# Taking the 32 largest scores from maxima of four instead of maxima of two

## The chip, the cores and the metric

The kernel runs on one core of a Trainium2 chip. The metric is device time in microseconds of one execution; lower is better. A core has five engines with queues of their own: TensorE (PE, matrix products), VectorE (DVE), ScalarE (ACT), GpSimd (POOL) and SyncE (SP, which issues most transfers). [...]

## The reference, cut to what matters

A gated cross-attention block over 8 batches of 512 text rows, with 1024 context rows per batch, four heads of width 32, is followed by a state-space mixing, a feed-forward layer and a routed layer of eight experts. The change touches only how attention picks its scores:

```
scores = einsum("bthd,bghd->bhtg", Q, K) / sqrt(32)      # 8 x 4 x 512 rows of 1024
topv, topi = top_k(scores, 32)
probs = softmax(topv)
attn = zeros_like(scores).at[..., topi].set(probs)
attn_mean = attn.mean(over heads)
```

Per row of 1024 scores one needs the 32nd largest value (the threshold), the largest one (for the exponent), and the sum of the exponentials of those at or above the threshold.

## The kernel before, in words

The rows of a batch are four tiles of 128 rows (t), one row per partition. A step of attention treats one tile and two heads, i = 0 and 1: 8 batches x 4 tiles x 2 pairs of heads are 64 steps, or 128 heads of one tile. In a step ScalarE copies the scores of the two heads from PSUM into tiles sc[0] and sc[1] of 128 x 1024 float32. Then the selection follows:

- VectorE takes the maximum of the left and the right half of a score row (line 943), 512 pair maxima, into the first half of a tile mn.
- GpSimd finds the smaller one of each pair: it adds the two halves as 32-bit whole numbers (line 945) and subtracts the maximum (line 946). The result is the bit pattern of the minimum, in the second half of mn.
- VectorE draws the 32 largest pair maxima in four rounds of MAX8 (the eight largest of a row), with MATCH_REPLACE8 between them (those eight replaced by a very low number, line 956, in a tile left).
- One MAX8 over the 512 pair minima (line 965) takes their eight largest. The eighth largest of these eight and of the last eight of the first 32 is the threshold th. It is the right one as long as no more than eight of a row's 32 are pair minima.

Afterwards ScalarE has made the exponentials e of all scores; VectorE multiplies them with (score >= threshold) and sums them (line 977, an operation with two SBUF tiles as inputs); ScalarE counts the chosen ones through a sum of signs, scales by the reciprocal of the sum, and GpSimd adds the heads up in acc (line 984). At the end of the program the counts are looked at: if a row has not exactly 32, a general version of the whole computation runs behind.

Buffers set part of the order: two tiles mn, two left and two e for all steps, so that a step's mn becomes free with the MAX8 over its second half, and four score tiles.

Beside the attention of batch b, the mixing, feed-forward and routed work of batch b - 1 runs on the same engines. The kernel does not write its instructions out in the order of the program: it notes them all with an estimated cost (function `time`, line 137) and their dependencies and buffers, and a list planner (function `order`, line 220) puts them into each engine's queue by estimated start and then by place in the program, shifted for attention and scores by the constants of line 337. So each engine's order is fixed before the kernel runs and follows estimates, not the chip. In TensorE's planned gaps the kernel puts filler matmuls (idle). Every planned instruction is recorded under line 326 in the profile; the tiles' names tell them apart: mn, left, top (the maxima drawn), t (the last MAX8 of 16), e, acc, sc.

Of the kernel before, what the change touches and what calls it, by code (L numbers as in the profile page):

```python
# [12 lines left out]
F32 = mybir.dt.float32  # L13
# [3 lines left out]
I32 = mybir.dt.int32  # L17
AF = mybir.ActivationFunctionType
ALU = mybir.AluOpType
# [3 lines left out]
P = 128  # L23
# [326 lines left out]
def tile_kernel(ctx: ExitStack, tc: tile.TileContext, a: dict, out: bass.AP):  # L350
# [3 lines left out]
    G, DV = cx.shape[1:]  # L354
    H, DH = 4, 32
    KTOP = 32
    HID = a["L0_xattn_W1"].shape[1]
    NST = a["L0_xattn_A_re"].shape[1]
    NE, _, NI = a["L0_ffn_rt_gate"].shape
# [4 lines left out]

    L = T // 2
    NL, NFFT = L // P, 2 * L
    SCALE = 1.0 / float(np.sqrt(np.float32(DH)))


# [15 lines left out]
    pk = ctx.enter_context(tc.tile_pool(name="pk", bufs=2))  # L385
# [10 lines left out]
    V, S, GP, TE, SY = (plan.engine(n, e) for n, e in (  # L396
        ("DVE", nc.vector), ("ACT", nc.scalar), ("POOL", nc.gpsimd), ("PE", nc.tensor), ("SP", nc.sync)))
# [495 lines left out]
    def scores(b, s, t, h0):  # L893

        plan.lead += LEAD_S
        n = f"{b}_{t}_{h0}"
        sc = [pq.tile([P, G], F32, tag="s", name=f"sc{n}_{i}") for i in range(2)]
        for q in range(G // 512):
            qs = slice(q * 512, (q + 1) * 512)
            pS = []  # L900
            for i in range(2):
                hp = slice((h0 + i) * DH, (h0 + i + 1) * DH)
                pS.append(ps_sc.tile([P, 512], F32, tag="sc", name=f"pS{n}_{i}_{q}", bufs=2))
                TE.matmul(pS[i], s.qT[hp, t * P : (t + 1) * P], s.kT[hp, qs], start=True, stop=True)
            for i in range(2):
                S.copy(sc[i][:, qs], pS[i])
        plan.lead -= LEAD_S
        return sc

    def attention(states):  # L910


        steps = [(b, t, h0) for b in range(B) for t in range(NT) for h0 in range(0, H, 2)]
        ahead = scores(0, states[0], 0, 0)
        behind = None
        for k, (b, t, h0) in enumerate(steps):
            s, sc = states[b], ahead
            if k + 1 < len(steps):
                b_, t_, h_ = steps[k + 1]
                for _ in states[b_].prep:  # L920
                    pass
                ahead = scores(b_, states[b_], t_, h_)
            if (t, h0) == (0, 0):


                s.uT = pk.tile([DK + 1, 2, T], F32, tag="uT", name=f"uT{b}")
                GP.memset(s.uT[DK : DK + 1, 0, :], 1.0)
            if h0 == 0:
                acc = pk.tile([P, G], F32, tag="acc", name=f"acc{b}_{t}")
            n = f"{b}_{t}_{h0}"  # L930

            top = pk.tile([P, 2, KTOP + 8], F32, tag="top", name="top" + n)
            sm = pk.tile([P, 5, 2], F32, tag="sm", name="sm" + n)
            nm, nb, na, su, ri = (sm[:, k_, :] for k_ in range(5))
            e_, mn = [], []
            for i in range(2):
                m_ = pk.tile([P, 2, G // 2], F32, tag="mn", name=f"mn{n}_{i}")  # L940
                mn.append(m_)
                lo, hi = sc[i][:, : G // 2], sc[i][:, G // 2 :]
                V.tensor_tensor(m_[:, 0], lo, hi, ALU.max)
                mi = m_.bitcast(I32)
                GP.tensor_tensor(mi[:, 1], lo.bitcast(I32), hi.bitcast(I32), ALU.add)
                GP.tensor_tensor(mi[:, 1], mi[:, 1], mi[:, 0], ALU.subtract)
            for i in range(2):
                for r in range(KTOP // 8):
                    t8 = top[:, i, r * 8 : r * 8 + 8]
                    src = mn[i][:, 0] if r == 0 else left  # L950
                    V.max(t8, src)
                    if r == 0:
                        S.activation(nm[:, i : i + 1], t8[:, 0:1], AF.Copy, scale=-SCALE)
                        left = pk.tile([P, G // 2], F32, tag="left", name=f"left{n}_{i}")
                    if r < KTOP // 8 - 1:
                        V.match_replace(left, t8, src, TAKEN)
                e_.append(pk.tile([P, G], F32, tag="e", name=f"e{n}_{i}"))
                S.activation(e_[i], sc[i], AF.Exp, bias=nm[:, i : i + 1], scale=SCALE)
                if i == 0:
                    yield  # L960
                    if behind is not None:
                        behind()
                        behind = None
            for i in range(2):
                V.max(top[:, i, KTOP:], mn[i][:, 1])
            t8 = pk.tile([P, 2, 8], F32, tag="t8", name="t8" + n)
            for i in range(2):
                V.max(t8[:, i, :], top[:, i, KTOP - 8 :])
            th = t8[:, :, 7]

            S.activation(na, th, AF.Abs, scale=EPS32)
            for i in range(2):
                S.activation(nb[:, i : i + 1], th[:, i : i + 1], AF.Identity, bias=na[:, i : i + 1],
                             scale=-1.0)
            for i in range(2):
                c = (b * NT + t) * H + h0 + i
                V.scalar_tensor_tensor(e_[i], sc[i], th[:, i : i + 1], e_[i], ALU.is_ge, ALU.mult,
                                       accum_out=su[:, i : i + 1])
                S.activation(junk, sc[i], AF.Sign, bias=nb[:, i : i + 1], accum_out=cnt[:, c : c + 1])
            V.reciprocal(ri, su)  # L980
            for i in range(2):
                S.activation(acc if h0 + i == 0 else e_[i], e_[i], AF.Copy, scale=ri[:, i : i + 1])
                if h0 + i:
                    GP.tensor_add(acc, acc, e_[i])
            if h0 + 2 == H:
                behind = partial(weighted, b, s, t, acc)
            yield
        behind()

    def attention_masked(b, s):  # L990
# [3 lines left out]
        for t in range(NT):  # L994
            acc = pk.tile([P, G], F32, tag="acc", name=f"acc{b}_{t}")
            for h in range(H):
# [14 lines left out]
                for r in range(KTOP // 8):  # L1011
                    src = sc if r == 0 else wk_
                    V.max(top[:, r * 8 : r * 8 + 8], src)
                    if r == 0:
                        GP.tensor_scalar(sm[:, 0:1], top[:, 0:1], -SCALE, None, ALU.mult)
                    V.match_replace(wk_, top[:, r * 8 : r * 8 + 8], src, TAKEN)

                S.activation(top, top, AF.Exp, bias=sm[:, 0:1], scale=SCALE, accum_out=sm[:, 1:2])
                S.activation(sc, sc, AF.Exp, bias=sm[:, 0:1], scale=SCALE)
                S.activation(wk_, wk_, AF.Exp, bias=sm[:, 0:1], scale=SCALE)  # L1020
                GP.tensor_sub(sc, sc, wk_)
# [353 lines left out]
    for _ in states[0].prep:  # L1375
        pass
    att = plan.ahead(attention(states), LEAD_A)
    def behind(b):

        s_, between, n = mixed(b, states[b]), (), n_mix + n_mlp  # L1380
        rows = None
        if b - 1 in TAKE:
            k = TAKE[b - 1]
            if b == B - 1:
                rows = [rows_of(blk[b - 1], i, f"{b - 1}_{i}", "xb" if i < 2 else "left")
                        for i in range(k)]
            k0 = max(0, k - BETWEEN)
            if k0:
                s_ = beside((s_, n_mix), (routed(b - 1, 0, k0, rows), k0))
            between = routed(b - 1, k0, k, rows)  # L1390
            n += k
        return chain([s_, after_mix(b, states[b], between)]), n
# [96 lines left out]
```

## Time and profile before

| | us |
|---|---|
| median of three runs | 1891.26 (1880.09 to 1892.16) |
| the profiled execution | 1877.53 |
| its span, first to last instruction | 1875.8 |
| PE busy, filler matmuls in it | 1712.8, 380.7 |
| DVE busy | 1465.7 |
| ACT busy | 1173.7 |
| POOL busy | 1089.6 |

A group of instructions in the profile is given as line, engine, operation, out<-in, shapes and count, then busy time in us, the mean of one in ns, and the idle time of the engine just before them with what ended it. In the order of time a line has the start in us, the length in us, engine and operation. A line of waits has who waited, for whom, and then the total in us, the number and the longest.

### The profile page before, as it was taken

The numbers are of one execution on the slowest core, as the hardware profiler recorded it, in microseconds if no ns is written. First come the engines' busy times: TensorE is split into PE (matmuls) and PEld (weight loads), VectorE is DVE, ScalarE is ACT, GpSimd is POOL, SyncE is SP. The second block draws the span as 40 slices with busy tenths as digits, with TensorE's granted clock in tenths as the row PEclk, the third lists the DMA queues.
The fourth block names the chain that finished last, engine by engine and source line by source line (L and its number), as shares of the span: only waits on it lengthen the run. The fifth ranks groups of instructions, "written<-read, shape, count | busy, mean of one in ns | idle before, by whom it ended". The sixth has DMA issues, their size and how long they took to land. (4 is left out here: it accounts for less than half of the span.)

```text
span 1875.8 us, 24133 instructions
## 1 busy us (share of the span) xinstructions
PE 1712.8 (91%) x7888; PEld 992.7 (53%) x7888; DVE 1465.7 (78%) x2841; ACT 1173.7 (63%) x2020; POOL 1089.6 (58%) x1048
## 2 busy tenths in 40 slices
PE   8588997999989988999889889988999999999996
PEld 3254453445544554575447444654466546547685
DVE  4999988898889887989778989788998999531210
ACT  5577745577747764798469756976697678413221
POOL 5454435665765665577655856585758677532122
PEclk9799998999999988999989999998999999999998
DMA  4000010001100120044003320233013305532694
GB/s 113 0 1 23 20 46 17 1 12 57 57 17 12 56 62 17 23 132 127 17 12 115 94 79 12 71 111 107 12 49 104 118 1 148 170 118 76 188 289 127
DMA packets 101301, 131.88 MB, mean 70 GB/s; under 512 B 9687, under 2 KB 73004, under 8 KB 101166
## 3 DMA queue, kind: packets, MB, share of 16 engines
q1 hardware_dynamic: 93102, 121.05, 20.6%
q0 software_dynamic: 7008, 8.42, 2.6%
q8 instruction: 64, 1.05, 0.2%
q10 hardware_dynamic: 1056, 0.79, 0.1%
q14 instruction: 71, 0.58, 0.1%
HBM read 112.22 MB, written 18.78 MB: 70 GB/s over the span
## 5 line engine op out<-in xcount | busy, mean ns | idle before, releaser
L1409 PE MATMUL idle<-ones 128*128 128x512 bf16 x1525 | 380.7, 392 | 0.0
L326 POOL TENSOR_TENSOR acc<-acc,e 128x1024 f32<-128x1024 f32 x96 | 233.0, 2428 | 134.4 <-ACT e L326 131.9
L326 POOL TENSOR_TENSOR mn<-sc 128x512 int32<-128x512 int32 x128 | 204.0, 1603 | 155.3 <-DVE top L326 97.1
L326 DVE MAX8 top<-left 128x8 f32<-128x512 f32 x384 | 265.5, 691 | 10.4
L1409 PEld LDWEIGHTS <-ones 128*128 128x128 bf16 x1525 | 149.2, 101 | 197.6 <-issue 64.7
L326 DVE SCALAR_TENSOR_TENSOR e<-sc,t,e 128x1024 f32<-128x1024 f32 x128 | 210.3, 1660 | 18.2 <-ACT e L326 18.2
L326 PE MATMUL pS<-kT,qT 32*128 32x512 f32 x512 | 209.7, 663 | 13.9 <-ACT sc L326 13.4
L326 POOL TENSOR_TENSOR mn<-mn 128x512 int32<-128x512 int32 x128 | 180.8, 1424 | 64.7 <-DVE mn L326 61.4
L326 ACT COPY sc<-pS 128x512 f32<-128x512 f32 x256 | 142.8, 584 | 85.2 <-PE pS L326 65.9
L326 DVE MATCH_REPLACE8 left<-top,left 128x512 f32<-128x512 f32 x256 | 172.9, 675 | 0.0
L326 ACT ACT_TABLE_LOAD x130 | 166.8, 1283 | 7.8 <-PE p L326 2.1
L326 DVE MAX8 top<-mn 128x8 f32<-128x512 f32 x256 | 169.2, 679 | 3.0 <-POOL mn L326 2.7
L326 DVE TENSOR_TENSOR mn<-sc 128x512 f32<-128x512 f32 x128 | 150.1, 1198 | 24.8 <-ACT sc L326 24.8
L326 ACT ACTIVATE e<-sc,sm 128x1024 f32<-128x1024 f32 x128 | 146.1, 1148 | 30.7 <-POOL acc L326 27.2
L326 ACT ACTIVATE junk<-sc,sm 128x1024 bf16<-128x1024 f32 x128 | 146.3, 1143 | 1.3
L326 PE MATMUL pu<-aT,cx 128*96 128x128 f32 x1024 | 131.1, 277 | 0.9 <-ACT aT L326 0.9
L326 PEld LDWEIGHTS pu<-aT,cx 128*96 128x96 f32 x1024 | 119.5, 165 | 21.9 <-issue 15.2
L326 POOL DMA_INDIRECT out_dram<-yb,to x38 | 65.8, 1732 | 105.2 <-DMA out_dram<-yb,to 50.0
L326 PE MATMUL pm<-hT,w 128*128 128x512 f32 x256 | 119.1, 598 | 0.3
L326 PE MATMUL am<-w,ga 128*128 128x256 f32 x512 | 117.5, 380 | 2.0 <-ACT ga L326 2.0
L326 ACT ACTIVATE e<-e,sm 128x1024 f32<-128x1024 f32 x96 | 108.7, 1151 | 3.8 <-DVE sm L326 3.7
L326 PEld LDWEIGHTS pS<-kT,qT 32*128 32x128 f32 x512 | 57.7, 189 | 96.8 <-ACT sc L326 48.9
(288 smaller groups left out, 3165.8 us busy)
## 6 DMA issues: line engine op xcount, KB each, us to landing
rt_gate<-in_L_ffn_rt_gate_dram SPq DMA_DIRECT2D x38, 512.0 KB, 4.9
rt_up<-in_L_ffn_rt_up_dram SPq DMA_DIRECT2D x38, 512.0 KB, 3.7
rt_down<-in_L_ffn_rt_down_dram SPq DMA_DIRECT2D x38, 512.0 KB, 4.7
w<-in_L_xattn_W_dram SPq DMA_DIRECT2D x32, 512.0 KB, 4.1
cx<-in_ctx_dram SPq DMA_DIRECT2D x7, 768.0 KB
xtab<-zt SPq DMA_DIRECT2D x8, 642.5 KB, 4.1
xb<-xtab SPq DMA_DIRECT2D x38, 128.5 KB, 4.3
xt<-in_x_dram SPq DMA_DIRECT2D x8, 512.0 KB, 3.8
```

Source lines behind the costliest of these rows:

```text
L326: o.fn()
L1409: nc.tensor.matmul(idle, ones16, bc(ones16, 1, 4), start=True, stop=True)
```

## The change

The score row is now seen as 256 groups of four (columns g, g + 256, g + 512, g + 768), Q = 256. VectorE first takes the 512 pair maxima of both heads as before. Then, per head, it takes the maximum of the two pair maxima of each group into a tile hi (256 columns, in the buffer that left had). GpSimd makes the pair minima with the same add and subtract, into columns 512 to 1023 of mn. Behind that VectorE puts the smaller of the two pair maxima into columns 256 to 511 of mn, in place. Columns 256 to 1023 of mn are then the three scores of each group that are not its highest.

The four rounds of MAX8 and the three of MATCH_REPLACE8 run over the 256 group maxima; the first round reads hi, and MATCH_REPLACE8 writes into columns 0 to 255 of mn, which the later rounds use. One MAX8 over the other 768 columns takes the place of the one over 512. The threshold is right as long as no more than eight of a row's 32 are not the highest of their group.

```diff
     L = T // 2
     NL, NFFT = L // P, 2 * L
+    Q = G // 4
...
-            e_, mn = [], []
+            e_, mn, hi = [], [], []
             for i in range(2):
-                m_ = pk.tile([P, 2, G // 2], F32, tag="mn", name=f"mn{n}_{i}")
+                m_ = pk.tile([P, G], F32, tag="mn", name=f"mn{n}_{i}")
                 mn.append(m_)
-                lo, hi = sc[i][:, : G // 2], sc[i][:, G // 2 :]
-                V.tensor_tensor(m_[:, 0], lo, hi, ALU.max)
-                mi = m_.bitcast(I32)
-                GP.tensor_tensor(mi[:, 1], lo.bitcast(I32), hi.bitcast(I32), ALU.add)
-                GP.tensor_tensor(mi[:, 1], mi[:, 1], mi[:, 0], ALU.subtract)
+                V.tensor_tensor(m_[:, : 2 * Q], sc[i][:, : 2 * Q], sc[i][:, 2 * Q :], ALU.max)
             for i in range(2):
+                m_ = mn[i]
+                hi.append(pk.tile([P, Q], F32, tag="left", name=f"hi{n}_{i}"))
+                V.tensor_tensor(hi[i], m_[:, :Q], m_[:, Q : 2 * Q], ALU.max)
+                mi, si = m_.bitcast(I32), sc[i].bitcast(I32)
+                GP.tensor_tensor(mi[:, 2 * Q :], si[:, : 2 * Q], si[:, 2 * Q :], ALU.add)
+                GP.tensor_tensor(mi[:, 2 * Q :], mi[:, 2 * Q :], mi[:, : 2 * Q], ALU.subtract)
+                V.tensor_tensor(m_[:, Q : 2 * Q], m_[:, :Q], m_[:, Q : 2 * Q], ALU.min)
+            for i in range(2):
+                left = mn[i][:, :Q]
                 for r in range(KTOP // 8):
                     t8 = top[:, i, r * 8 : r * 8 + 8]
-                    src = mn[i][:, 0] if r == 0 else left
+                    src = hi[i] if r == 0 else left
                     V.max(t8, src)
                     if r == 0:
                         S.activation(nm[:, i : i + 1], t8[:, 0:1], AF.Copy, scale=-SCALE)
-                        left = pk.tile([P, G // 2], F32, tag="left", name=f"left{n}_{i}")
                     if r < KTOP // 8 - 1:
                         V.match_replace(left, t8, src, TAKEN)
...
             for i in range(2):
-                V.max(top[:, i, KTOP:], mn[i][:, 1])
+                V.max(top[:, i, KTOP:], mn[i][:, Q:])
```

## The prediction

> **What bounds the kernel now.** I read the engines' busy shares, then busy time by stage, then VectorE's groups, the waits, and last the order in time on VectorE and GpSimd. The whole-span shares put TensorE first, but 380.7 us of its 1712.8 are the filler matmuls that the plan puts into planned gaps, and the chain that ended last only describes the last 170 us. The stages say more: attention runs from 34 to 1608 us.
>
> ```profile
> 34.00:1608.00 1574.00, 1445.27 (x6498) 804.78 (x6498) 1395.59 (x2668) 1095.99 (x1862) 998.53 (x904) 0.95 0.18 52
> 1608.00:1876.00 268.00, 242.22 (x1290) 175.04 (x1288) 59.92 (x144) 61.76 (x119) 75.03 (x102) 0.96 0.53 166
> ```
>
> Columns after the length: busy us of TensorE, weight loads, VectorE, ScalarE, GpSimd. VectorE is busy for 1395.6 of 1574.0 us (89%). The rest is about 149 us in gaps over 0.15 us (its waits below, summed in that window) and about 30 us of small seams. TensorE without filler has 1147 us there, ScalarE 1096, GpSimd 999. So attention, 64 steps of two heads at 24.6 us, moves at VectorE's pace; the 268 us behind it hold no selection.
>
> ```profile
> L326 DVE MAX8 top<-left 128x8 f32<-128x512 f32 x384 | 265.5, 691 | 10.4
> L326 DVE SCALAR_TENSOR_TENSOR e<-sc,t,e 128x1024 f32<-128x1024 f32 x128 | 210.3, 1660 | 18.2 <-ACT e L326 18.2
> L326 DVE MATCH_REPLACE8 left<-top,left 128x512 f32<-128x512 f32 x256 | 172.9, 675 | 0.0
> L326 DVE MAX8 top<-mn 128x8 f32<-128x512 f32 x256 | 169.2, 679 | 3.0 <-POOL mn L326 2.7
> L326 DVE TENSOR_TENSOR mn<-sc 128x512 f32<-128x512 f32 x128 | 150.1, 1198 | 24.8 <-ACT sc L326 24.8
> L326 DVE TENSOR_TENSOR us<-us 128x256 f32<-128x256 f32 x8 | 3.4, 425 | 0.2
> L326 POOL TENSOR_TENSOR mn<-sc 128x512 int32<-128x512 int32 x128 | 204.0, 1603 | 155.3 <-DVE top L326 97.1 <-ACT sc L326 35.6 <-DVE t L326 12.8
> ```
>
> After the bar: busy us, mean ns of one, idle before. The one-input operations have one length whatever runs beside them (MAX8 624 to 699 ns). The two that read two SBUF tiles do not: the pair maximum has a median of 688 ns and a mean of 1198, the e product a shortest of 1249 and a mean of 1660. The order in time shows why (start us, us):
>
> ```profile
> 615.29 2.37 POOL L326 TENSOR_TENSOR acc<-acc,e 128x1024 f32<-128x1024 f32 x1
> 616.07 2.14 DVE L326 TENSOR_TENSOR mn<-sc 128x512 f32<-128x512 f32 x1 [0.18 <-ACT sc L326]
> 617.60 1.74 POOL L326 TENSOR_TENSOR mn<-sc 128x512 int32<-128x512 int32 x1
> ```
>
> VectorE's maximum starts under GpSimd's add, ends 0.55 us after it, and GpSimd's next add is then 0.47 us longer than its usual 1.27. Last the waits:
>
> ```profile
> DVE top L326 <- POOL mn L326: 2.7, 3, 1.2
> POOL mn L326 <- DVE top L326: 97.1, 27, 14.5
> ```
>
> VectorE waited 2.7 us in all for GpSimd's minima, needed only at a head's end; GpSimd waits for VectorE to free the mn buffers, so its two instructions often start just when the next maximum does.
>
> [...]
>
> **The change part by part**, per head, of which there are 128.
>
> (1) Four MAX8 and three MATCH_REPLACE8 go from 512 to 256 columns. MAX8 is 168 ns at 16 and 691 at 512, so 1.054 ns a column: 421 at 256. MATCH_REPLACE8, with the same slope, 676 - 270 = 406. Saved: 4 x 0.270 + 3 x 0.270 = 1.89 us.
> (2) The MAX8 over the rest goes from 512 to 768 columns: 0.679 to about 0.96, +0.28.
> (3) Two new VectorE operations of 256 columns (maximum and minimum of the pair maxima) at 0.425 clean: +0.85, and two seams of 0.03: +0.06.
> Sum with nobody on the port: -1.89 + 0.28 + 0.85 + 0.06 = -0.70 us a head, -90 us for 128.
> (4) But both new ones read two SBUF tiles, and VectorE's exposed operations go from two a head to four. The price of exposure is in two rows: 1198 - 688 = 0.51 us for the maximum, 1660 - 1267 (its tenth percentile) = 0.39 for the product. Break-even for each new one is 0.70/2 = 0.35. Lower bound 0 (each falls into a GpSimd gap; a gain from the port is excluded), upper bound 1.2, nearly a whole 1.27 us add each time. I take 0.51: the new maximum comes when the GpSimd add of the same head is due, and the minimum right after GpSimd's subtract, as the next GpSimd instruction starts. So +1.02 a head.
> (5) The new edge. The minimum overwrites what GpSimd's subtract reads, and the first MATCH_REPLACE8 overwrites what the minimum reads. So from the second round the chain stands behind GpSimd's add and subtract, 1.27 + 1.27 clean, 1.60 + 1.42 as measured, which had a whole selection's time before. Queued behind a waiting minimum on VectorE is everything: the other head, the e products, the earlier batch's products, for which ScalarE and TensorE wait. Cover: the other head's maxima (0.69 + 0.42), two MAX8 (0.84), the e products (1.27 each) and some 5 us a step of the earlier batch; that is enough if the planned order mixes them in. I price it at nothing; uncovered, it is up to 2.5 us a step, 160 us. Below nothing is excluded: no wait is removed.
> (6) Moved: GpSimd's 256 instructions keep their widths and stand behind both maxima in the program, one place later; no DMA and nothing of SP's queue moves. The buffer hi is the old left at half its width. ScalarE's work is the same, its scale of the top value after 0.27 us less. The planner's costs give 0.68 us to a two-input operation of 256 columns and so expect a gain; its order is made for that.
>
> Sum: 128 x (-0.70 + 1.02) = +41 us. The profiled execution took 1877.5 us (span 1875.8 plus 1.7), 13.7 under the median of the three runs. 1877.5 + 41 = 1918.5; in terms of the median, 1932.
>
> **The rivals.** (B) Faster: the order puts MAX8 and the earlier batch's PSUM operations under GpSimd's instructions, and the new operations meet a free port. For it: 74 of the 128 pair maxima now are within 0.1 us of clean. At 0.1 to 0.2 us each the head gains 0.4, 50 us: 1840. It decides below 0.35 each. Against: the new ones come in the very microseconds when GpSimd works on the same tiles. (C) Slower by much: the step start becomes an alternation. Walk, both buffers free at 0: maximum to 0.69; add to 1.82; second maximum held to 2.4; subtract to 3.5; hi held to 3.8; second add to 4.95; second hi held to 5.25; second subtract to 6.4; minimum held to 6.7. That is 2.65 us of work in 6.7, a loss of 4 us where the old order lost 1.2 (the second maximum alone). 2.8 more a step, less the 1.4 saved, is 90 us: 1980. For it: 27 waits of GpSimd for the freed buffer set up this start. Against: a second maximum often comes later (612.17 and 616.07 here), and one-input work lies between. (D) No change: 0.3 to 0.4 us of port time each, or the saved time goes to what VectorE waits for now (43.6 us for the film products): 1891. That the change misses and the general program behind the last check runs too is excluded: counted from the reference's scores on these inputs, no row has more than 7 of its 32 outside the highest of its groups of four, and the one step takes 8.
>
> **How the numbers follow.** Mine (+20 to +65 us) 0.42, B 0.32, C 0.12, D 0.14. 1% is about what a measurement here can tell from no change (the three runs span 0.6%). A part of mine near +20 lies in "same". Faster 0.32, same 0.17, slower 0.51. Predicted 1932. The range reaches to B at its centre and to C at its: 1838 to 1980; my case alone, 1911 to 1956.
>
> **What would show it.** Right: MAX8 at 421 and 960 ns, MATCH_REPLACE8 at 406; new tensor_tensor rows of 256 columns with means of 0.8 to 1.0 us against minima near 0.42; the GpSimd rows longer than 1603 and 1424; waits of VectorE's mn for GpSimd's mn below 20 us; VectorE's busy time in attention some 40 us up. Wrong: means under 0.75 for the new rows (B), or VectorE waits on GpSimd of over 60 us (C). A reshuffled plan of the film waits could move 20 us either way and would fit none of the cases.

## The result and the profile after

The changed kernel takes 1958.9 us in the median (1955.0 to 1961.7, four runs), the kernel before 1885.9 in the runs measured beside it and earlier ones: a ratio of 1.0383, with a 95% interval of 1.0349 to 1.0417. The change costs 73 us; the forecast was 1932 (+41), slower by the same mechanism, with the size short by 32 us. The 73 us lie inside the whole range, but above the +20 to +65 us of the forecast's own case and below the +90 us of rival C. Two profiled executions are compared here: spans of 1875.8 and 1953.3 us.

The stages after, read as before (attention up to the last e product, then the rest; length and then busy us of TensorE, weight loads, VectorE, ScalarE, GpSimd; the last three columns are TensorE's granted clock, the transfers' share and GB/s):

```profile
33.00:1687.00 1654.00, 1487.57 (x6481) 824.06 (x6480) 1420.88 (x2928) 1096.64 (x1865) 1018.20 (x904) 0.93 0.17 50
1687.00:1954.00 267.00, 241.88 (x1292) 175.78 (x1292) 54.43 (x141) 60.39 (x114) 74.73 (x102) 0.96 0.53 166
```

All of it is in attention. From the first pair maximum to the last e product it takes 1653.3 us against 1577.0. In that stretch VectorE is busy for 1420.7 instead of 1399.1 us (+21.6) and idle for 232.6 instead of 177.9 (+54.7). So nearly three quarters of the loss are idle time, not work. Of the 54.7 us, waits that GpSimd ended are 31.2 (from 25.5 to 56.7), waits that TensorE ended 14.5 (69.6 to 84.1), and gaps under 0.15 us are 8.0. VectorE's groups after (busy us, mean ns, idle before):

```profile
L326 DVE SCALAR_TENSOR_TENSOR e<-sc,t,e 128x1024 f32<-128x1024 f32 x128 | 204.2, 1610 | 15.9 <-ACT e L326 15.3
L326 DVE MAX8 top<-mn 128x8 f32<-128x256 f32 x384 | 163.5, 426 | 11.5
L326 DVE TENSOR_TENSOR hi<-mn 128x256 f32<-128x256 f32 x128 | 136.1, 1074 | 0.3
L326 DVE TENSOR_TENSOR mn<-sc 128x512 f32<-128x512 f32 x128 | 128.7, 1030 | 18.0 <-ACT sc L326 18.0
L326 DVE TENSOR_TENSOR mn<-mn 128x256 f32<-128x256 f32 x128 | 120.4, 942 | 33.2 <-POOL mn L326 28.0
L326 DVE MAX8 top<-mn 128x8 f32<-128x768 f32 x128 | 116.9, 943 | 0.0
L326 DVE MATCH_REPLACE8 mn<-top,mn 128x256 f32<-128x256 f32 x256 | 104.5, 408 | 0.0
L326 DVE MATCH_REPLACE8 mn<-top,hi 128x256 f32<-128x256 f32 x128 | 52.3, 408 | 0.0
L326 DVE MAX8 top<-hi 128x8 f32<-128x256 f32 x128 | 51.8, 412 | 0.1
```

The rows of MAX8 and MATCH_REPLACE8 sum to 489.0 us, against 694.1 before (the three rows shown with the prediction, and the first round's MATCH_REPLACE8):

```profile
L326 DVE MATCH_REPLACE8 left<-top,mn 128x512 f32<-128x512 f32 x128 | 86.5, 676 | 0.0
```

So 205 us are saved, and every length is within 5% of its forecast. The two new operations take 256.5 us, 2.4 times their clean 0.425 us each. The wait on the second one, for GpSimd's subtract, is new. Step by step (start us, length us; VectorE's maximum of two groups shown as x2):

```profile
922.91 1.27 DVE L326 TENSOR_TENSOR mn<-sc 128x512 f32<-128x512 f32 x2
924.10 1.49 DVE L326 TENSOR_TENSOR hi<-mn 128x256 f32<-128x256 f32 x1
925.70 1.31 DVE L326 TENSOR_TENSOR mn<-mn 128x256 f32<-128x256 f32 x1
926.93 0.41 DVE L326 TENSOR_TENSOR hi<-mn 128x256 f32<-128x256 f32 x1
927.26 0.68 DVE L326 TENSOR_TENSOR ger<-sgr,pu 128x512 f32<-128x512 f32 x1
927.86 0.41 DVE L326 TENSOR_TENSOR mn<-mn 128x256 f32<-128x256 f32 x1
```

and GpSimd in the same microseconds:

```profile
923.72 3.00 POOL L326 TENSOR_TENSOR mn<-mn 128x512 int32<-128x512 int32 x2 [3.95 <-DVE mn L326]
```

The two subtracts end at 925.31 and 926.72. The first hi (1.49) ends 0.28 us after the first of them and the first minimum (1.31) 0.29 us after the second; the second pair, placed behind both, takes 0.41 each.

All 256 new operations show the same. The trace has 53 that no GpSimd instruction overlaps, and they take 401 to 426 ns. It has 140 longer than 500 ns, and 138 of these end 0.27 to 0.31 us after a GpSimd instruction does: they were held until it was through. Over the clean length they lose about 152 us in all: 84 directly behind one of GpSimd's adds and subtracts, 48 behind a sum in acc, the rest behind smaller instructions.

The kernel before shows the same. Of its 128 pair maxima the 54 longer than 0.79 us all end 0.546 to 0.560 us after a GpSimd instruction. MAX8, with one input, shows none of it: of the 384 over left, 255 run while GpSimd works and take 635 to 697 ns, the other 129 take 624 to 699. This holding is what the prediction and the expectations call the port; the traces show its lengths and not what in the chip makes it.

### The profile page after: what moved, and what is told of

It is laid out like the page before. It is cut to its first block, busy times and chain, and to the rows that moved or that the text cites. A ratio compares the mean times of both kernels' runs of the same rounds, so it can differ in the third digit from the quotient of the medians.

```text
span 1953.3 us, 24453 instructions
## 1 busy us (share of the span) xinstructions
PE 1754.0 (90%) x7875; PEld 1012.9 (52%) x7875; DVE 1485.5 (76%) x3097; ACT 1173.3 (60%) x2019; POOL 1108.9 (57%) x1048
## 5 line engine op out<-in xcount | busy, mean ns | idle before, releaser
L326 POOL TENSOR_TENSOR mn<-sc 128x512 int32<-128x512 int32 x128 | 202.2, 1588 | 210.9 <-DVE top L326 122.6
L326 DVE MAX8 top<-mn 128x8 f32<-128x256 f32 (+1 forms) x512 | 275.6, 555 | 11.5
L326 PE MATMUL pS<-kT,qT 32*128 32x512 f32 x512 | 219.4, 688 | 24.7 <-ACT sc L326 24.2
L326 POOL TENSOR_TENSOR mn<-mn 128x512 int32<-128x512 int32 x128 | 183.9, 1447 | 68.2 <-DVE mn L326 66.3
L326 DVE SCALAR_TENSOR_TENSOR e<-sc,t,e 128x1024 f32<-128x1024 f32 x128 | 204.2, 1610 | 15.9 <-ACT e L326 15.3
L326 DVE TENSOR_TENSOR mn<-mn 128x256 f32<-128x256 f32 x128 | 120.4, 942 | 33.2 <-POOL mn L326 28.0
L326 PE MATMUL pu<-aT,cx 128*96 128x128 f32 x1024 | 137.0, 284 | 6.4 <-ACT aT L326 6.3
L326 DVE TENSOR_TENSOR mn<-sc 128x512 f32<-128x512 f32 x128 | 128.7, 1030 | 18.0 <-ACT sc L326 18.0
L326 DVE TENSOR_TENSOR hi<-mn 128x256 f32<-128x256 f32 x128 | 136.1, 1074 | 0.3
L326 PE MATMUL am<-w,ga 128*128 128x256 f32 x512 | 122.6, 393 | 12.5 <-ACT ga L326 12.4
L326 POOL TENSOR_TENSOR yf<-yf,t 128x512 f32<-128x512 f32 (+1 forms) x80 | 91.2, 1166 | 54.2 <-DVE t L326 40.8
L326 PEld LDWEIGHTS am<-w,ga 128*128 128x128 f32 x512 | 98.7, 196 | 37.9 <-ACT ga L326 17.9
L326 PEld LDWEIGHTS pS<-kT,qT 32*128 32x128 f32 x512 | 60.6, 195 | 110.9 <-ACT sc L326 54.7
```

Source lines behind the costliest of these rows:

```text
L326: o.fn()
```

## The experiments

The theory, in the expectations the port theory: the two new operations, which read two SBUF tiles each, are held until a GpSimd instruction has ended, as 138 of the 140 long ones were, and the minimum ties the selection to GpSimd's subtract. The rivals: the wait alone; the planned order, since an edit of costs and dependencies moves nearly every instruction; TensorE's clock, which was 0.935 in the profile after against 0.955. Ratios are to the kernel before, run on the same chip beside each. The edge is the dependency by which the chain of MAX8 and MATCH_REPLACE8 waits for GpSimd's subtract.

| kernel | median us | ratio (95%) |
|---|---|---|
| changed | 1958.9 | 1.0383 (1.0349 to 1.0417) |
| e1 no edge | 1949.0 | 1.0334 (1.0288 to 1.0381) |
| e2 no edge, one-input operations | 1835.6 | 0.9749 (0.9694 to 0.9805) |
| e3 no minimum | 1905.2 | 1.0106 (1.0068 to 1.0144) |
| e4 planner's price | 1933.9 | 1.0258 (1.0231 to 1.0286) |
| e5 edge, one-input operations | 1876.4 | 0.9964 (0.9941 to 0.9987) |
| e6 before, no pair minima | 1820.4 | 0.9656 (0.9600 to 0.9711) |
| e7 changed, no pair minima | 1793.9 | 0.9498 (0.9453 to 0.9543) |
| e8 more filler | 1955.9 | 1.0361 (1.0314 to 1.0408) |
| e9 no minimum, last MAX8 over 512 | 1880.8 | 0.9975 (0.9957 to 0.9994) |
| e10 as e9, no edge | 1856.3 | 0.9846 (0.9816 to 0.9875) |
| e11 no edge, planner's price | 1930.3 | 1.0240 (1.0209 to 1.0271) |
| e12 as e2, one tile | 1863.9 | 0.9892 (0.9840 to 0.9945) |

**The edge and the holding, one by one.** e1 takes the edge away (with it, the pair maxima get a tile of their own, which is free earlier than mn was):

```diff
-                m_ = pk.tile([P, G], F32, tag="mn", name=f"mn{n}_{i}")
+                m_ = pk.tile([P, 2 * Q], F32, tag="mn", name=f"mn{n}_{i}")
...
+                rest.append(pk.tile([P, 3 * Q], F32, tag="rest", name=f"rest{n}_{i}"))
...
-                GP.tensor_tensor(mi[:, 2 * Q :], si[:, : 2 * Q], si[:, 2 * Q :], ALU.add)
-                GP.tensor_tensor(mi[:, 2 * Q :], mi[:, 2 * Q :], mi[:, : 2 * Q], ALU.subtract)
-                V.tensor_tensor(m_[:, Q : 2 * Q], m_[:, :Q], m_[:, Q : 2 * Q], ALU.min)
+                GP.tensor_tensor(ri_[:, Q:], si[:, : 2 * Q], si[:, 2 * Q :], ALU.add)
+                GP.tensor_tensor(ri_[:, Q:], ri_[:, Q:], mi, ALU.subtract)
+                V.tensor_tensor(rest[i][:, :Q], m_[:, :Q], m_[:, Q : 2 * Q], ALU.min)
...
-                left = mn[i][:, :Q]
+                left = hi[i]
...
-                V.max(top[:, i, KTOP:], mn[i][:, Q:])
+                V.max(top[:, i, KTOP:], rest[i])
```

> The same operations as the changed kernel, but the minimum goes into a tile of its own beside the pair minima, and MATCH_REPLACE8 works in hi in place, so that nothing on VectorE waits for GpSimd's subtract before the last MAX8. If the wait (the new edge) is the main loss: the 28 us of waits of VectorE's mn for GpSimd's mn go, and some of the shifted waits with them: 1900 to 1915. If the shared port is the main loss: hi and the minimum stay at means of 0.9 to 1.1 us and the time stays at 1925 to 1945, only the 28 us of waits less. If neither, but the new planned order: any value near 1959, with other waits.

Measured 1949.0, 4 us above the port theory's band. That is 10 us less than the changed kernel, and the two intervals overlap: taking the edge away alone shows no clear effect. The group of the minimum says where its waits went:

```profile
L326 DVE TENSOR_TENSOR rest<-mn 128x256 f32<-128x256 f32 x128 | 152.3, 1190 | 0.0
L326 DVE TENSOR_TENSOR hi<-mn 128x256 f32<-128x256 f32 x128 | 129.6, 1013 | 0.5
```

No idle time before it any more, but 1190 instead of 942 ns. Freed of the wait, the new operations are held behind GpSimd instead: 141 of the 143 longer than 500 ns end 0.27 to 0.31 us after a GpSimd instruction, 89 of them after an add or subtract. The rival "the wait alone" falls.

e2 is e1 with the two operations as reductions over pairs, which have one SBUF input:

```diff
-                V.tensor_tensor(hi[i], m_[:, :Q], m_[:, Q : 2 * Q], ALU.max)
+                V.tensor_reduce(hi[i], m_[:, : 2 * Q].rearrange("p (h q) -> p q h", h=2), AX.X, ALU.max)
...
-                V.tensor_tensor(rest[i][:, :Q], m_[:, :Q], m_[:, Q : 2 * Q], ALU.min)
+                V.tensor_reduce(rest[i][:, :Q], m_[:, : 2 * Q].rearrange("p (h q) -> p q h", h=2), AX.X, ALU.min)
```

> As the kernel without the edge, but the maximum and the minimum of the pair maxima are reductions over pairs with one SBUF input of 512 elements each. If the shared port is the loss: both have one length of about 0.69 us (together 1.38 against the 2.02 of the changed kernel, 0.63 a head, 81 us), and GpSimd's instructions are shortened: 1855 to 1885, level with or a little below the kernel before. If the port is not the loss but the order of the plan, it gains what its lengths give over 0.85 us of clean work, that is nothing: 1925 to 1960.

Measured 1835.6: 113 us less than e1, and 2.5% (1.9 to 3.1) faster than the kernel before. It is 19 us below the port theory's band, so the gain is larger than was expected.

```profile
L326 DVE TENSOR_REDUCE rest<-mn 128x256 f32<-128x512 f32 x128 | 87.6, 684 | 0.0
L326 DVE TENSOR_REDUCE hi<-mn 128x256 f32<-128x512 f32 x128 | 87.5, 684 | 0.5
```

They read 512 elements each and have 1.6 times the clean length of the two-input form, yet together 0.84 us less a head than in e1 (1.37 against 2.20), 107 us for 128. The selection does the same thing in both. So the form decided the case: with two SBUF inputs 141 of the 256 new operations were held behind GpSimd (e1), with one input none shows it (e2, 659 to 709 ns in all 256 places).

This pair also answers the rival of the planned order. The planner gives the reduction 0.68 us, as it gives the two-input form, so it makes nearly the same plan: of VectorE's 3097 instructions 96% have, by their tiles' names, the same place in the queue in e1 and e2. Between the changed kernel and e1 it is only about half. The other comparisons here move the plan as well, and their small differences are less certain for it.

e5 puts the edge back into e2; one line is different, so that the second round of the selection waits for GpSimd's subtract:

```diff
-                left = hi[i]
+                left = mn[i][:, :Q]
```

> The kernel with one-input reductions for the two new operations, and with the edge put back: MATCH_REPLACE8 writes its first result over the left quarter of the pair maxima again, which GpSimd's subtract reads, so the second round waits for GpSimd. If the edge costs as little as the run without it said (10 us): 1836 to 1855. If its price was hidden there because the time went over to the port: 1865 to 1900, with waits of VectorE's mn for GpSimd's rest of over 40 us.

Measured 1876.4, 41 us more than e2. VectorE's busy time in attention hardly rises (1351.6 against 1338.4), its idle time does: 236.4 against 194.8. Of these 41.6 us, waits that GpSimd ended are 32.1. The one that was forecast is there, but shorter than the 40 us that were named:

```profile
DVE mn L326 <- POOL rest L326: 26.3, 17, 6.3
```

So the edge has a price when the new operations are not held (685 ns each in e5), which e1 could not show. But the line does two things: it ties VectorE to the subtract, and it holds the buffer of the pair maxima longer. e12 holds the buffer without the tie, with pair maxima and rest in one tile of 5 * Q columns again.

> The kernel with one-input reductions and without the edge (1836 us), but the pair maxima and the rest stand in one tile again, so that the next step's pair maximum waits for the last MAX8 of this one, as in the changed kernel. It separates what the edge run (1876 us) put together: the wait for GpSimd's subtract and the longer hold of the buffer. If the wait for GpSimd is what costs: 1828 to 1846. If the hold of the buffer costs: 1860 to 1885.

Measured a ratio of 0.9892 (1863.9 us), between the two and in the band of the hold. So the hold alone costs some 0.014 (27 us). The waits show where: VectorE's wait for ScalarE's exponentials is 10.6 us in e2 and 38.8 in e12.

```profile
DVE e L326 <- ACT e L326: 10.6, 9, 2.8
DVE e L326 <- ACT e L326: 38.8, 16, 9.2
```

In e5, which holds the buffer nearly as long, most of the added idle time is waits for GpSimd. So the two prices are not plainly parts of one sum. The tie costs between 14 us (e12 to e5, whose intervals touch) and 41 us (e2 to e5), and no run parts it from the changed plan. The hold is nothing new, since the kernel before has it too; e1 and e2 had lifted it by the way.

**GpSimd's two instructions left out.** e6 and e7 leave GpSimd's add and subtract out of both kernels. A memset of the same columns stands in their place, no pair minimum takes part in the selection, and the check of the counts is left out (the lines are e7's).

```diff
-                GP.tensor_tensor(mi[:, 2 * Q :], si[:, : 2 * Q], si[:, 2 * Q :], ALU.add)
-                GP.tensor_tensor(mi[:, 2 * Q :], mi[:, 2 * Q :], mi[:, : 2 * Q], ALU.subtract)
+                GP.memset(m_[:, 2 * Q :], TAKEN)
...
-    V.tensor_scalar(cnt, cnt, float(2 * KTOP - G), None, ALU.is_equal)
-    V.tensor_reduce(ok[:, 0:1], cnt, AX.X, ALU.min)
+    V.memset(ok[:, 0:1], 1.0)
```

> The kernel before with GpSimd's add and subtract left out; a memset of the same 512 columns to a very low number, which reads no SBUF, stands in their place. So the pair minima take no part, the thresholds of some rows are wrong, and the check of the counts with the general program is left out. The pair maximum and the e product lose their waits for those two instructions (about 18 and 40 us of the 118 in the kernel before): 1815 to 1850 by the port theory; 1870 to 1890 if those waits were not on the path.

> The changed kernel with the same left out: no pair minima, a memset of the 512 columns, no check of the counts. If GpSimd's two instructions on the port are what turns the change from a gain into a loss: faster than the kernel before with the same left out, by 50 to 90 us (0.70 us a head clean, less some waits for the sums in acc), 1750 to 1790. If the loss is the planned order or VectorE is no longer the limit: within 20 us of that kernel or slower.

Measured 1820.4, in the port theory's band, and 1793.9, just above it: with GpSimd's two instructions gone, the change is 26.6 us faster than its counterpart, where it was 73 slower. The sign turns, as the port theory said, but the size lies between the two bands (50 to 90, or within 20). The new operations in e7:

```profile
L326 DVE TENSOR_TENSOR hi<-mn 128x256 f32<-128x256 f32 x128 | 75.1, 587 | 0.3
L326 DVE TENSOR_TENSOR mn<-mn 128x256 f32<-128x256 f32 x128 | 72.8, 569 | 3.5
```

1074 + 942 falls to 587 + 569 ns: 0.86 us a head, 110 us in all, went with GpSimd's add and subtract. In the changed kernel 84 us were lost directly behind those two; in e7 the losses behind the sums in acc are smaller as well (28 us against 48). The memset removes the edge too, and the plan is another. The gain is about half of the least that was expected. VectorE's busy time in attention is 53 us under e6's, but its idle time is 33 us over it (250.0 against 217.1).

**The minimum left out.** e3 deletes the minimum from the changed kernel and leaves the check of the counts out (the last MAX8 reads the second quarter as it is).

> The changed kernel without the minimum of the pair maxima: the last MAX8 reads the pair maxima's second half as it is, so the threshold is wrong in some rows, and the check of the counts and so the general program behind it is left out. If the port is the loss: 128 times the mean 0.94 us go, 120 us of VectorE's time, and 28 us of waits move to MATCH_REPLACE8, which still waits for the subtract: 1845 to 1870. If the new order of the plan is the loss: only the clean 0.43 us go, 55 us: 1900 to 1915.

Measured 1905.2, a miss for the port theory, and inside the band of the rival, the planned order. Yet its reason, that only the clean 55 us of work go, does not hold: VectorE's busy time in attention fell by 109 us, as the port theory has it, and its idle time rose by 69. The wait for the subtract has moved to MATCH_REPLACE8 (38.9 us), and the e product waits 54.5 us for the exponentials. To see whether the edge, which is still there at MATCH_REPLACE8, caused that, e9 is e3 with the last MAX8 over the pair minima alone, and e10 is the same without the edge (by the edit of e1).

> The changed kernel without the minimum of the pair maxima, as in the earlier run of that kind, and the last MAX8 over the 512 pair minima alone (0.68 instead of 0.94 us). The thresholds of some rows are wrong; the check of the counts is left out. MATCH_REPLACE8 still waits for GpSimd's subtract. The earlier run lost 109 us of VectorE's busy time in attention and gained only 54. If the edge holds the selection up: again only part of 128 x 0.26 = 33 us is gained, 1885 to 1905. If that run was held up by something else: 1865 to 1880.

> The same work as the run with the last MAX8 over 512 columns and no minimum, the same left out, but without the edge: MATCH_REPLACE8 works in hi in place and GpSimd's result is needed at the head's end alone. If the edge is what kept VectorE's saved time from showing: 30 to 60 us faster than that run, 1830 to 1865. If the edge is nearly free beside the port, as the first run without it had it: within 15 us of that run.

Measured 1880.8 and 1856.3: e9 lies between its two bands, and the 24.5 us from e9 to e10 (with the buffer's hold in them) lie between "nearly free" (within 15) and the 30 to 60 of the other case. So the two runs do not decide it. And e10's VectorE is still idle for 275 us in attention, so the edge explains the smaller part. Its waits name the rest:

```profile
DVE xm L326 <- PE pfi L326: 53.5, 16, 9.8
DVE e L326 <- ACT e L326: 51.1, 18, 7.0
```

The wait of xm, work of the batch before, for TensorE's film product pfi is no longer than in the kernel before (54.5). The e product waits 51.1 us for ScalarE's exponentials, 18.2 in the kernel before. So with VectorE's work 113 us under that of the kernel before, only 26 us of time are won. Other engines' results come late, and VectorE is no longer the only limit. Why the exponentials come late was not settled; no run moved ScalarE's order alone.

**The planned order and the clock.** e4 changes nothing in the changed kernel but the planner's price of a two-input SBUF operation of 256 columns, and e11 does the same in e1.

```diff
-                t = 0.07 + 0.0012 * width + (0.0 if psum else 0.1 + 0.0008 * width)
+                t = 0.07 + 0.0012 * width + (0.0 if psum else 0.63 if width == 256 else 0.1 + 0.0008 * width)
```

> The changed kernel with one constant of the planner changed: an operation of 256 columns with SBUF inputs is given 1.0 us as measured in the changed kernel, in place of 0.68. If the loss is an order planned on a wrong price: 1890 to 1920. If it is the port and the wait themselves: 1945 to 1975, since the new price moves no instruction off the port.

> The kernel without the edge, with 1.0 us as the planner's price of an operation of 256 columns with SBUF inputs (measured there 1.0 and 1.2). In the changed kernel the price was worth 25 us. If the price makes the planner put the two operations where the port is free: 1905 to 1930, with means under 0.9 us. If it only makes the planned wait fit the real one: 1935 to 1955, and means as before.

Measured 1933.9 and 1930.3: 25 us less than the changed kernel, 19 less than e1. e4 lies between its two bands, e11 at the upper edge of its first. In e11 hi and the minimum have means of 1082 and 1095 ns, against 1013 and 1190: with the price they are held as long as before, 2177 ns together against 2203. A part of the loss, about a third of the 73 us, goes with an order planned on 0.68 us for what takes 1.0; two thirds stay. From e11, whose plan has a price near the measured length, to e2 it is still 95 us.

e8 fills TensorE's planned gaps up to 24 us fully (`FILL_MAX, FILL, STEP = 24.0, 1.0, 0.22`).

> The changed kernel with all of TensorE's planned gaps filled with filler matmuls (share 1.0 instead of 0.85, gaps up to 24 us instead of 12). TensorE's granted clock in the profile was 0.935 against 0.955 before. If the lower clock is part of the cause: 1925 to 1945 at a clock of 0.95. If it only follows from the longer waits: 1950 to 1975, whatever the clock.

Measured 1955.9, with a clock of 0.949 in the profile. VectorE, ScalarE and GpSimd have their instructions in the same order as in the changed kernel. Most of the clock comes back, the time does not. So the lower clock is not what cost the 73 us; that it follows from the waits is likely, and not shown.

## Why the prediction was right, and what was mis-sized

The likeliest case was right in sign, and in the holding behind GpSimd as the main loss; it was wrong on the edge. By its steps:

(1) and (2), the narrower selection: forecast -1.61 us a head, 206 us; measured 205.

(3) and (4), the two new operations beside GpSimd: forecast 2 x (0.425 + 0.51), 239 us; measured 256.5 us, 0.65 and 0.52 us over the clean length. The shown cause is e1 against e2, and e6 against e7. The step named GpSimd's add and subtract alone; in the changed kernel 48 of the 152 us are lost behind the sums in acc. Its second price, 0.39 for the e product, is a mean less a tenth percentile; less the median (1421), as for the maximum, it is 0.24 (the sum used 0.51). What the sum left out is that the older two-input operations would lose less: the pair maximum fell from 1198 to 1030 ns, the e product from 1660 to 1610, 28 us together. That the new operations took their collisions is a likely reason, and not shown. So VectorE's busy time in attention rose by 21.6 us, not by 41.

(5), the edge, is the mis-sized term. I priced it at nothing, covered by other work. VectorE waits 28.0 us for the subtract at the minimum alone, and all waits in attention that GpSimd ended rose from 25.5 to 56.7 us. With one-input operations the tie costs 14 to 41 us (e12 and e2 against e5), and from e10 to e9 it is 24.5 with the hold of the buffer in it. The cover was there in kind but not at the time: each engine's order is fixed, and in those 28.0 us (16 waits) VectorE ran nothing. At 614.48 us of the trace a minimum starts after 1.16 us of such idle time; the other head's hi, whose pair maximum was done by 613.0, starts behind it, at 615.88.

(6) I took the planner's price of 0.68 us as a hint that it expects a gain, and not as an error with a price. e4 puts that at 25 us.

The busy time was forecast too high and the idle time at next to nothing, when it rose by 54.7 us. The two errors have opposite signs, so the total of 41 came nearer to 73 than its terms deserve: that is luck. The 14.5 us of added waits for TensorE were in no step; the film product has 11 of them, and their cause stays open.

The ratios make a sum of their own: the narrower selection with one-input operations in e12, 0.9892, 20 us faster; from there to e5, with the tie, +0.0072, 14 us; from there to the changed kernel's two-input operations +0.0419, 79 us; together +0.0383, the 72 us that the ratio measured. Each of these kernels has a plan of its own, which e4 shows can be worth 25 us. e5 and the changed kernel also differ in the rest's own tile, which frees the pair maxima at the last round instead of at the last MAX8; so the 79 us may hold a little of that.

Rival B (new operations that are not held) is what e2 sets up, and there the change wins. Rival C (an alternation at the start of a step) can be seen where the changed kernel's step at 922.9 us was shown, but for one head of two, so its 4 us a step were not reached. Its mark, waits on GpSimd of over 60 us, was nearly met with 56.7: the change ended between my case and C. Of the marks named for my case, four were missed: VectorE's wait for GpSimd's mn was 28.0 us, not below 20; GpSimd's add took 1588 ns, no longer than before (its subtract 1447 against 1424, longer); busy time rose by half as much as said; and of the means of the new rows 0.94 us is in the named 0.8 to 1.0, 1.07 above it. The lengths of MAX8 and MATCH_REPLACE8 were as named.

## What to carry to other kernels

Before adding a short two-input VectorE operation beside GpSimd work, price it with its collisions: the mean minus the median of the pair maximum already there gave 0.51 us each, measured 0.65 and 0.52 for an operation of 0.425. If the same thing can be said as a reduction with one SBUF input, its longer length can be cheaper where it stays fixed (0.68 us, 659 to 709 ns in e2, against 1.0 us). With the edge kept, that took the change from a loss of 73 us to level with the kernel before (e5, 0.9964); with the edge and the buffer's hold lifted too, it wins 49 (e2). And an edge from a slow engine into the middle of a chain is not free because other work exists: here it was priced at nothing, and VectorE waited 28.0 us at it. Where the order is fixed, ask what stands behind the waiting instruction.

## What the runs showed that was not expected

Taking a wait away can leave the time where it was because the instruction is then held behind GpSimd: in e1 the 28 us of waits were gone, and each of 128 minima took 0.25 us more, 32 us.

The time follows VectorE's work only in part. From the kernel before to e6, e7 and e10 its busy time in attention falls by 97, 150 and 113 us, and attention gets shorter by 58, 78 and 16 us. From e1 to e2 it was the whole: 96 us of work, 117 of time.

Two operations of a fixed length (684 ns, 659 to 709) did better than two of 425 ns clean, with VectorE's queue in nearly the same order: the shorter form was held behind GpSimd in more than half of its places (141 of 256 in e1).

TensorE's granted clock fell (0.955 to 0.935) in the slower kernel and was brought to 0.949 by filler without a gain.
